# GpSimd normalises per chunk of tokens: one two-scalar operation instead of two broadcast operations, with the planner's constants that go with it

## The chip, the cores and the metric

The kernel runs on one core of a Trainium2 chip. The metric is the device time of one execution in microseconds (us); lower is better. The engines are TensorE (PE, with its weight load PEld), VectorE (DVE), ScalarE (ACT), GpSimd (POOL) and SyncE (SP, which issues DMAs).

## The reference

The input x has 32 sequences of 256 tokens with 128 features. Three residual steps follow one another: a feed-forward network at half weight, an attention, and the same feed-forward network again.

```
x = x + 0.5 * ffn(layernorm(x))
x = x + attn(layernorm(x))          # 16 heads of 8 features; inside: layernorm(ctx + x) * gamma + beta
x = x + 0.5 * ffn(layernorm(x))
```

The ffn has three layers, 128 (with its negative) to 512, 512 to 512 and 512 to 128, whose weights are +1 or -1, with a ReLU after the first two. The layernorm subtracts the mean of a token and multiplies with `rsqrt(var + eps)`. So every token is normalised four times: ahead of the first ffn, ahead of the attention, inside the attention, and ahead of the second ffn.

## The kernel before

The work is cut into 16 units of 512 tokens (two sequences each). A unit is a tile of 128 partitions by 4 chunks by 128 features; a chunk is 128 tokens, one to a partition. For each unit `u` the kernel calls `norm_first` and `first` (norm and first ffn), `norm_attn` and `project` (norm, query, key and value), then for each of its two sequences `b` `maxima` and `shift` (scores and their row maximum), `weigh` (scores again, exponential, product with the values) and `context` (division, residual, the inner layernorm), and last `second` (norm, second ffn, store). In the ffn every hidden value is held as a sum of two fp16 numbers, high and low (`relu_split`, lines 661 to 667).

None of these functions issues an instruction at once. Each calls `op`, which notes a node with its engine, a cost, what it reads and writes, and a rank. `_Plan.simulate` then plays all nodes through a list scheduler and writes down one fixed order for each engine; the chip runs that order. The rank is the due time of a node in score steps: a unit has 16 ranks (`UNIT`), because it has 16 groups of score matmuls, one a rank. The constants at the top of the file enter there:

- `B0`, `BA`, `BP`, `BW`, `B1`, `P0`, `P1`, `P2`, `BB`, `AHEAD`, `RUSH`: the rank at which each part of a unit starts.
- `TURN_X`, `TURN_C`: TensorE's transposes get an even rank plus this number (line 632 for the normalised tile, line 921 for the context).
- `SKIP0`, `SKIP`, `UNTIL`: score groups run strictly by rank. Other TensorE work may be taken ahead of its turn, up to `SKIP0` ranks ahead of the oldest group left, and up to `SKIP` ranks once that group's rank passes `UNTIL` (line 243).
- `CAST`, `BIAS`, `BIAS2`: costs and thresholds by which a `relu_split` is turned from DVE to POOL. In `relief`, ACT writes the ReLU a second time in fp32 (`full`, line 666) and POOL subtracts (line 661). In `divert`, ACT writes only `full` (line 667), and POOL makes the high part (CAST, line 667) and the low part (line 661).
- `QF`, `QK`, `QL`: for which units the normalising is `quick`, that is, done on DVE: the first ffn of units below `QF`, the attention norm of units below `QK`, and the context and second ffn of the last `QL` units.

TensorE has three ways of cutting its array: score groups use four row strips ("R"), the product with the values four column strips ("C", lines 877 and 423), the transposes the whole array ("D", lines 420, 630, 921). The ffn and projection products (kind "F", function `dense`) take the cut that is set at that moment: L423 in strips, L420 whole.

`normalize` (lines 590 to 618) first takes the statistics of each chunk on DVE (L603, L604: mean and variance into `mv`), then on POOL `ve = (var + eps) / scale^2` (L605) and `rs = ve ^ -0.5` (L607). If not `quick`, POOL then does the whole tile in two operations with broadcast operands (L617 subtracts the means, L618 multiplies with `rs`); it works on 4 chunks in the ffn and attention norms (tiles `fxn`, `axn`, 128x512) and on 2 in the context (tile `z`, 128x256). If `quick`, DVE does one operation for each chunk with two scalars per partition (L612), and `ve` and `rs` are made for two chunks at a time. `turned` then transposes the tile (L630) and splits it (L633, L634).

Of the kernel before, what the change touches and what calls it, by code (L numbers as in the profile page):

```python
# [41 lines left out]
ALU = mybir.AluOpType  # L42
# [7 lines left out]
EPS = 1e-5  # L50
# [4 lines left out]

PT, NXN = 5, 5

QF, QK = 1, 1

QL = 1  # L60

UNIT = 16
B0, BA, BP, BW, BV, B1 = -30, -10.627, -6.547, 13, 4, 42.462

P0, P1, P2, SLOW = 16.003, 17.354, 16, 1

TURN_X, TURN_C = 1.5, 1.5  # L70

WARM = 14

BB = 15.813

RUSH, AHEAD = -0.12, 4.08

SKIP0, SKIP, UNTIL = 10.311, 2.868, 28.215

FAR = 19.64  # L80

HOLD = (0, 0.0, 0.0)

CAST = 1.0

WAIT = 0.057

# [4 lines left out]

AFTER, REACH = (0.165, 0.085, 0.11, 0.04, 0.0), (0.053, 0.033, 0.037, 0.08, 0.05)

BIAS = 1.115

BIAS2 = 0.714
PE, DVE, ACT, POOL, SP = range(5)


# [19 lines left out]
class _Plan:  # L120
# [11 lines left out]
    def op(self, eng, cost, emit, r=(), w=(), rank=0.0, kind="D", rows=0, lag=None, alt=None, rush=False):  # L132
        x = _Node()
        x.n, x.eng, x.cost, x.emit, x.rank, x.kind, x.rows = len(self.nodes), eng, cost, emit, rank, kind, rows
        x.lag, x.alt, x.tiling = lag, alt, "D"
        x.then, x.avail, x.start, x.rush = [], 0.0, None, rush
        x.pair = None
        needs = set()
        for k in r:
            if k in self.wrote:  # L140
                needs.add(self.wrote[k])
        for k in w:
            if k in self.wrote:
                needs.add(self.wrote[k])
            needs.update(self.read.pop(k, ()))
        for k in r:
            self.read.setdefault(k, []).append(x)
        for k in w:
            self.wrote[k] = x
        needs.discard(x)  # L150
        x.needs = list(needs)
        for y in x.needs:
            y.then.append(x)
        x.bufs = []
        for k in (*r, *w):
            b = k[0] if isinstance(k, tuple) else k
            if isinstance(b, _Buf) and b not in x.bufs:
                x.bufs.append(b)
                b.left += 1
        self.nodes.append(x)  # L160
        return x

    def simulate(self):
# [12 lines left out]
        def fits(x, also=()):  # L176
            want = {}
            for b in (*x.bufs, *also):
                if not b.held:
                    want.setdefault(b.tag, set()).add(b)  # L180
            return all(used.get(tag, 0) + len(bs) <= next(iter(bs)).bufs for tag, bs in want.items())
# [86 lines left out]
        def relief(now, best):  # L268

            nonlocal left  # L270
            for x in sorted((x for x in ready[DVE] if x.alt and x.avail <= now + 1e-9), key=lambda x: (x.rank, x.n)):
# [5 lines left out]
                other = max(now + act + 0.2, max(free[POOL], now) + wait) + pool  # L277
                if other > max(free[DVE], now) + before + x.cost + BIAS:
                    continue
# [23 lines left out]
        def divert(x, now):  # L303
# [7 lines left out]
            wait = sum(y.cost for y in ready[POOL] if (y.rank, y.n) < (x.rank, x.n))  # L311
            if max(free[POOL], end + 0.2) + wait + cost + sub > max(free[DVE], end) + before + low.cost + BIAS2 or not fits(x, [full]):
                return
# [76 lines left out]
def tile_macaron(ctx: ExitStack, tc: tile.TileContext, x, Wq, bq, Wk, bk, Wv, bv, gamma, beta, k0, k1, k2, s0, s1, s2, out):  # L390
    nc = tc.nc
    plan = _Plan(tc)
    op = plan.op
    B, S, D = x.shape
# [16 lines left out]
    def buf(pool, shape, dt, tag, bufs, name):  # L411
        return _Buf(pool, shape, dt, tag, bufs, name)
# [12 lines left out]
    def bc(ap, n):  # L425
        return ap.broadcast_to([ap.shape[0], ap.shape[1], n])
# [67 lines left out]
    scale = const.tile([P, 3], F32, name="scale")  # L494
# [5 lines left out]
    def projections():  # L500
# [15 lines left out]
        s = lambda emit, w, rank=-700: op(SP, 0.42, emit, w=w, rank=rank, lag=4.5)  # L516
        v = lambda cost, emit, r, w, rank=B0 + BB: op(DVE, cost, emit, r=r, w=w, rank=rank)
        for i, (W, b) in enumerate(((Wq, bq), (Wk, bk), (Wv, bv))):
# [11 lines left out]
        def permute(dst, src, eng):  # L530
            to = dst.rearrange("p (r d c e) -> p c r d e", r=R, d=HD, c=2)
            of = src.rearrange("p (c r e d) -> p c r d e", c=2, r=R, e=2)
            for c in range(2):
                eng(to[:, c], of[:, c])

        op(ACT, 0.4, lambda: permute(pid, ident, nc.scalar.copy), r=["ident"], w=["pid"], rank=B0 + BB)
        op(PE, 0.2, lambda: nc.tensor.transpose(bp.t, bound, ident), r=["bound", "ident"], w=[bp], rank=B0 + BB + 0.1)
        v(0.2, lambda: nc.vector.tensor_reduce(top[:, 0:1], bp.t, AX.X, ALU.max), [bp], ["top"])
        v(0.1, lambda: nc.vector.tensor_scalar(top[:, 1:2], top[:, 0:1], 320.0, 1e-30, ALU.mult, ALU.max), ["top"], ["top"])
        op(POOL, 0.5, lambda: nc.gpsimd.tensor_tensor(top[:, 2:3], top[:, 1:2], nhalf[0:3, 0:1], ALU.pow), r=["top", "nhalf"], w=["top"], rank=B0 + BB)  # L540

        v(0.1, lambda: nc.vector.tensor_scalar(top[:, 3:4].bitcast(I32), top[:, 2:3].bitcast(I32), 0x7F800000, None, ALU.bitwise_and), ["top"], ["top"])
        v(0.1, lambda: nc.vector.tensor_scalar(diag, ident[0:3, 0:3], top[:, 3:4], None, ALU.mult), ["ident", "top"], ["diag"])
        op(PE, 0.2, lambda: nc.tensor.matmul(sp.t, ones, diag, start=True, stop=True), r=["ones", "diag"], w=[sp], rank=B0 + BB + 0.2)
        v(0.1, lambda: nc.vector.tensor_scalar(scale, sp.t, 2.0**13, None, ALU.mult), [sp], ["scale"])
        for i in range(3):
            op(ACT, 0.22, lambda i=i: nc.scalar.activation(ws[:, i, :], ws[:, i, :], AF.Identity, scale=scale[:, i : i + 1]), r=[("ws", i), "scale"], w=[("ws", i)], rank=B0 + BB)
        v(0.2, lambda: nc.vector.reciprocal(inv, scale[:, 0:2]), ["scale"], ["inv"])
# [41 lines left out]
    def normalize(dst, src, tag, n, rank, scale=1.0, quick=False):  # L590

        of = lambda: src[0].t[:, src[1] : src[1] + n]
        srcs = [(src[0], src[1] + t) for t in range(0, n, 2)]
        mv = buf(small, [P, n, 2], F32, f"mv{tag}", 4, f"mv_{tag}")
        ve = buf(small, [P, n], F32, f"ve{tag}", 4, f"ve_{tag}")
        rs = buf(small, [P, n, 1], F32, f"rs{tag}", 4, f"rs_{tag}")
        step = 2 if quick else n
        for a in range(0, n, step):
            part = slice(a, a + step)
            ts = range(a, a + step)  # L600
            for t in ts:
                st = buf(small, [P, 6], F32, f"st{tag}", 4, f"st_{tag}_{t}")
                op(DVE, 0.195, lambda t=t, st=st: nc.vector.bn_stats(st.t, of()[:, t, :]), r=[srcs[t // 2]], w=[st], rank=rank)  # L603
                op(DVE, 0.085, lambda t=t, st=st: nc.vector.bn_aggr(mv.t[:, t, :], st.t), r=[st], w=[(mv, t)], rank=rank)  # L604
            op(POOL, 0.27, lambda part=part: nc.gpsimd.tensor_scalar(ve.t[:, part], mv.t[:, part, 1], EPS, 1.0 / scale**2, ALU.add, ALU.mult),  # L605
               r=[(mv, t) for t in ts], w=[(ve, a)], rank=rank)
            op(POOL, 0.35 + 0.2 * step, lambda part=part: nc.gpsimd.tensor_tensor(rs.t[:, part, 0], ve.t[:, part], nhalf[:, part], ALU.pow),  # L607
               r=[(ve, a), "nhalf"], w=[(rs, a)], rank=rank)
        mvs = [(mv, t) for t in range(n)]
        if quick:  # L610
            for t in range(n):
                op(DVE, 0.26, lambda t=t: nc.vector.tensor_scalar(dst.t[:, t, :], of()[:, t, :], mv.t[:, t, 0:1], rs.t[:, t, :], ALU.subtract, ALU.mult),  # L612
                   r=[srcs[t // 2], (rs, t // 2 * 2), (mv, t)], w=[(dst, t)], rank=rank)
        else:
            dsts = [(dst, t) for t in range(n)]
            cost = 0.2 + 0.2 * n
            op(POOL, cost, lambda: nc.gpsimd.tensor_tensor(dst.t, of(), bc(mv.t[:, :, 0:1], D), ALU.subtract), r=[*srcs, *mvs], w=dsts, rank=rank)  # L617
            op(POOL, cost, lambda: nc.gpsimd.tensor_tensor(dst.t, dst.t, bc(rs.t, D), ALU.mult), r=[(rs, 0)], w=dsts, rank=rank)  # L618

    def turned(xn, tag, name, n, rank):  # L620

# [34 lines left out]
    def relu_split(hi, lo, m, ps, w, rank):  # L656
# [3 lines left out]
        def low(of):  # L660
            return lambda: nc.gpsimd.tensor_tensor(lo.t[:, m, :], of.t, hi.t[:, m, :], ALU.subtract)  # L661
# [4 lines left out]
           alt=(0.09 + w / 1280, lambda: nc.scalar.activation(full.t, ps.t, AF.Relu), ps, full, 0.1 + w / 500, low(full)))  # L666
        h.pair = (l, lambda: nc.scalar.activation(full.t, ps.t, AF.Relu), full, CAST * w / 512, lambda: nc.gpsimd.tensor_copy(hi.t[:, m, :], full.t),
                  0.1 + w / 500, low(full))
# [61 lines left out]
    def second(u, b):  # L730
# [3 lines left out]
        rank = at(u) + (b or 0) * UNIT / 2  # L734
        norm_ffn(("ffn1", u, b), (xs[u], part), n, rank - AHEAD, u >= NU - QL)
        dsts = ffn(("ffn1", u, b), (xs[u], part), n, rank, span * n / NT)
# [216 lines left out]
    for u in range(NU):  # L953
# [10 lines left out]
        for b in range(2):  # L964
            weigh(u, b)
            context(u, b, u >= NU - QL)
            if u == NU - 1:
# [34 lines left out]
```

## Time and profile before

| what | us |
|---|---|
| median of 3 runs (lowest, highest) | 687.96 (687.93, 688.52) |
| the profiled execution's own time | 689.46 |
| its span, first to last instruction | 687.6 |
| PE busy | 659.8 (96%) |
| DVE busy | 581.1 (85%) |
| ACT busy | 543.1 (79%) |
| POOL busy | 497.3 (72%) |
| mean granted TensorE clock | 0.995 |

The span is one execution as the hardware profiler saw it. The profiled execution is 1.50 us longer than the median, and 1.86 us of its time lie outside the span. A busy share is an average over the whole span; the stretches differ. An answer by windows gives the busy time of each engine in a stretch of the span. The chain of waits is the work that ended last, followed backwards.

### The profile page before, as it was taken

To read this page: it belongs to the slowest core of one execution; us is meant where nothing else is said; L and a number is where in the kernel's file an instruction comes from. 1 tells how busy PE (TensorE), PEld (TensorE's weight loads), DVE (VectorE), ACT (ScalarE), POOL (GpSimd) and SP (SyncE) were. 2 spreads that over 40 slices of the span, in tenths; PEclk is the share of its full clock that TensorE was granted. 3 is DMA by queue.
4 is the path that set the end of the run, shared out by engine and by line. 5 is a ranking of instruction groups with operands and counts; after the bars stand their busy time and mean duration, and the time that the engine had idled before them with its cause. 6 is when DMAs were issued, how large, how long until landed. Compare 5 with 4: busy or idle time off the path is not lost.

```text
span 687.6 us, 28926 instructions
## 1 busy us (share of the span) xinstructions
PE 659.8 (96%) x12596; PEld 344.6 (50%) x12596; DVE 581.1 (85%) x1194; ACT 543.1 (79%) x871; POOL 497.3 (72%) x685
## 2 busy tenths in 40 slices
PE   7998978999999999999999999999999999999996
PEld 4544533545455554555455454555445454544455
DVE  7789887998989798898979889897988888889484
ACT  3546887788889888888978888897889787868953
POOL 6875596688686868768686877868686785865643
PEclk9999998999999999999999999999999999999999
DMA  7222200203011030301102030200203021300000
GB/s 222 76 79 80 64 23 3 83 5 98 5 49 54 3 98 4 100 4 58 46 5 97 3 99 5 76 27 16 86 5 97 4 74 30 96 4 20 5 17 31
DMA packets 33391, 33.59 MB, mean 49 GB/s; under 512 B 4992, under 2 KB 29056, under 8 KB 33264
## 3 DMA queue, kind: packets, MB, share of 16 engines
q1 hardware_dynamic: 31520, 30.89, 14.3%
q8 instruction: 99, 1.62, 1.0%
q10 hardware_dynamic: 1744, 0.85, 0.4%
q14 instruction: 28, 0.23, 0.1%
HBM read 18.58 MB, written 13.14 MB: 46 GB/s over the span
## 4 chain that ended last, share of the span: by engine, by line
PE 82%; DVE 7%; ACT 4%; POOL 3%; DMA 2%; issue 1%; SPq 0%; ACTq 0%; POOLq 0%
PE p_None L423 18%; PE p L423 17%; PE cx L877 16%; PE sc L895 9%; PE p L420 6%; DVE nm L836 4%; PE p_None L420 3%; PE nat L825 3%; ACT pt L907 2%; PE tp L921 2%; PE pq L423 2%; PE pq L420 1%; PE pv L423 1%; PE t L630 1%; PE t_None L630 1%
## 5 line engine op out<-in xcount | busy, mean ns | idle before, releaser
L836 DVE TENSOR_REDUCE nm<-nat 128x4 f32<-128x1024 f32 x256 | 310.5, 1216 | 27.4 <-PE nat L825 22.0
L907 ACT ACTIVATE pt<-sc,esc 128x1024 f32<-128x1024 f32 x256 | 285.2, 1116 | 54.7 <-PE nat L825 45.2
L423 PEld LDWEIGHTS <-w 128*32 128x32 f16 x3976 | 97.4, 96 | 102.4 <-issue 28.9
L877 PE MATMUL cx<-pt,vaug 128*32 128x256 f32 x2048 | 137.2, 385 | 0.0
L895 PE MATMUL sc<-qs,ks 32*128 32x256 f16 x1024 | 103.2, 274 | 6.7 <-ACT pt L907 4.9
L825 PE MATMUL nat<-ks,qs 32*128 32x256 f16 x1024 | 101.7, 274 | 3.9 <-ACT pt L907 1.8
L877 PEld LDWEIGHTS cx<-pt,vaug 128*32 128x32 f32 x2048 | 58.6, 110 | 44.7 <-issue 12.3
L423 PE MATMUL p<-h1h,w 128*32 128x512 f16 x796 | 78.5, 383 | 0.0
L423 PE MATMUL p<-h1l,w 128*32 128x512 f16 x796 | 78.0, 380 | 0.0
L423 PE MATMUL p_None<-h1h_None,w 128*32 128x512 f16 x744 | 73.6, 382 | 0.1
L423 PE MATMUL p_None<-h1l_None,w 128*32 128x512 f16 x744 | 73.0, 379 | 0.0
L895 PEld LDWEIGHTS <-ks 32*128 32x128 f16 x1024 | 31.7, 92 | 75.0 <-issue 70.7
L661 POOL TENSOR_TENSOR h2l_None<-full,h2h_None 128x512 f16<-128x512 f32 x27 | 31.5, 1168 | 27.6 <-ACT full L666 27.3
L661 POOL TENSOR_TENSOR h2l<-full,h2h 128x512 f16<-128x512 f32 (+1 forms) x36 | 40.8, 1134 | 11.5 <-ACT full L666 10.8
L663 ACT ACTIVATE h1h<-p 128x512 f16<-128x512 f32 (+1 forms) x68 | 37.3, 577 | 13.6 <-PE p L420 9.0
L825 PEld LDWEIGHTS <-qs 32*128 32x128 f16 x1024 | 31.3, 92 | 29.7 <-issue 28.7
L663 ACT ACTIVATE h2h<-p 128x512 f16<-128x512 f32 (+1 forms) x56 | 32.3, 576 | 15.7 <-PE p L420 11.8
L664 DVE SCALAR_TENSOR_TENSOR h2l_None<-p_None,h2h_None 128x512 f16<-128x512 f32 x33 | 22.7, 687 | 25.7 <-ACT h2h_None L663 25.6
L420 PEld LDWEIGHTS <-w 128*128 128x128 f16 x326 | 30.1, 98 | 28.5 <-issue 10.5
L664 DVE SCALAR_TENSOR_TENSOR h1l<-p,h1h 128x512 f16<-128x512 f32 (+1 forms) x61 | 39.4, 663 | 1.1 <-ACT h1h L663 0.8
L663 ACT ACTIVATE h2h_None<-p_None 128x512 f16<-128x512 f32 x56 | 33.4, 596 | 6.0 <-PE p_None L420 4.9
L423 PE MATMUL p_None<-xT_None,w 128*32 128x512 f16 x480 | 35.4, 380 | 0.0
(163 smaller groups left out, 1471.7 us busy)
## 6 DMA issues: line engine op xcount, KB each, us to landing
dr<-qkhl SPq DMA_DIRECT2D x32, 256.0 KB, 2.0
qs<-dr SPq DMA_DIRECT2D x48, 128.0 KB, 3.3
ks<-dr SPq DMA_DIRECT2D x48, 128.0 KB, 2.6
out_dram<-x SPq DMA_DIRECT2D x15, 256.0 KB, 3.0
x<-in_L_attn_x_dram SPq DMA_DIRECT2D x14, 256.0 KB, 6.1
dm<-mr SPq DMA_DIRECT2D x32, 16.0 KB, 2.5
qs<-dm SPq DMA_DIRECT2D x32, 16.0 KB
qs<-nought SPq DMA_DIRECT2D x13, 32.0 KB
```

Source lines behind the costliest of these rows:

```text
L420: nc.tensor.matmul(to, w, of, start=start, stop=stop)
L423: nc.tensor.matmul(to[32 * r : 32 * r + 32], w[:, 32 * r : 32 * r + 32], of, start=start, stop=stop)
L630: nc.tensor.transpose(pt.t[:, bass.ts(t, P)], xn.t[:, t, :], ident)
L661: return lambda: nc.gpsimd.tensor_tensor(lo.t[:, m, :], of.t, hi.t[:, m, :], ALU.subtract)
L663: h = op(ACT, 0.09 + w / 1280, lambda: nc.scalar.activation(hi.t[:, m, :], ps.t, AF.Relu), r=[ps], w=[(hi, m)], rank=rank)
L664: l = op(DVE, 0.08 + w / 985, lambda: nc.vector.scalar_tensor_tensor(lo.t[:, m, :], ps.t, 0.0, hi.t[:, m, :], ALU.max, ALU.subtract), r=[p ...
L825: nc.tensor.matmul(nat.t[:, ii, qc, :], Q[32 * r : 32 * r + 32, g, b * S + qc * P : b * S + qc * P + P], K[32 * r : 32 * r + 32, g, b * S ...
L836: op(DVE, 1.141, lambda g=g, pr=pr, nat=nat: nc.vector.tensor_reduce(nm.t[:, :, 2 * pr : 2 * pr + 2, g].rearrange("p q i -> p i q"), nat.t ...
L877: nc.tensor.matmul(cx.t[32 * r : 32 * r + 32, g // 2, :], V[:, 2 * b + kc, 4 * (g // 2) + r, 16 * (g % 2) : 16 * (g % 2) + 32], pts[g, r / ...
L895: nc.tensor.matmul(sc.t[:, ii, kc, :], K[32 * r : 32 * r + 32, g, b * S + kc * P : b * S + kc * P + P], Q[32 * r : 32 * r + 32, g, b * S : ...
L907: op(ACT, 1.012, lambda pt=pt, sc=sc: nc.scalar.activation(pt.t, sc.t, AF.Exp, scale=esc), r=[sc, "esc"], w=[pt], rank=rank - RUSH, rush=True)
L921: nc.tensor.transpose(tp.t[:, qc, 8 * c : 8 * c + 8, :].rearrange("p h n -> p (h n)"), cxT.t[:, c, bass.ts(qc, P)], ident)
```

## The change

`normalize` loses its two-operation branch. POOL now does what DVE did in the quick branch, one operation for each chunk, `(x - mean) * rs` with the chunk's two scalars, and each writes its chunk alone, so that what reads a chunk waits for that chunk. The planner's cost of it is `EACH`. With it come other values of the planner's constants; they change ranks, thresholds and the set of quick units, and so the order of every engine's queue.

```diff
-QF, QK = 1, 1
-QL = 1
+QF, QK = 3, 1
+QL = 0
...
-B0, BA, BP, BW, BV, B1 = -30, -10.627, -6.547, 13, 4, 42.462
-P0, P1, P2, SLOW = 16.003, 17.354, 16, 1
-TURN_X, TURN_C = 1.5, 1.5
+B0, BA, BP, BW, BV, B1 = -30, -11.353, -5.977, 13, 4, 42.462
+P0, P1, P2, SLOW = 16.003, 17.354, 15.993, 1
+TURN_X, TURN_C = 0.5, 1.5
...
-BB = 15.813
-RUSH, AHEAD = -0.12, 4.08
-SKIP0, SKIP, UNTIL = 10.311, 2.868, 28.215
+BB = 16
+RUSH, AHEAD = 0.144, 4.08
+SKIP0, SKIP, UNTIL = 10.602, 2.868, 20.746
...
-CAST = 1.0
+CAST = 0.62
+EACH = 0.4
...
-BIAS = 1.115
-BIAS2 = 0.714
+BIAS = 1.143
+BIAS2 = 0.765
...
-            op(POOL, 0.27, lambda part=part: nc.gpsimd.tensor_scalar(ve.t[:, part], mv.t[:, part, 1], EPS, 1.0 / scale**2, ALU.add, ALU.mult),
+            op(POOL, 0.21, lambda part=part: nc.gpsimd.tensor_scalar(ve.t[:, part], mv.t[:, part, 1], EPS, 1.0 / scale**2, ALU.add, ALU.mult),
...
-        mvs = [(mv, t) for t in range(n)]
-        if quick:
-            for t in range(n):
-                op(DVE, 0.26, lambda t=t: nc.vector.tensor_scalar(dst.t[:, t, :], of()[:, t, :], mv.t[:, t, 0:1], rs.t[:, t, :], ALU.subtract, ALU.mult),
-                   r=[srcs[t // 2], (rs, t // 2 * 2), (mv, t)], w=[(dst, t)], rank=rank)
-        else:
-            dsts = [(dst, t) for t in range(n)]
-            cost = 0.2 + 0.2 * n
-            op(POOL, cost, lambda: nc.gpsimd.tensor_tensor(dst.t, of(), bc(mv.t[:, :, 0:1], D), ALU.subtract), r=[*srcs, *mvs], w=dsts, rank=rank)
-            op(POOL, cost, lambda: nc.gpsimd.tensor_tensor(dst.t, dst.t, bc(rs.t, D), ALU.mult), r=[(rs, 0)], w=dsts, rank=rank)
+        e, eng, cost = (DVE, nc.vector, 0.26) if quick else (POOL, nc.gpsimd, EACH)
+        for t in range(n):
+            op(e, cost, lambda t=t: eng.tensor_scalar(dst.t[:, t, :], of()[:, t, :], mv.t[:, t, 0:1], rs.t[:, t, :], ALU.subtract, ALU.mult),
+               r=[srcs[t // 2], (rs, t // step * step), (mv, t)], w=[(dst, t)], rank=rank)
```

## The prediction

> **What bounds the kernel now.** I read the page first (busy shares and slices), then the busy time by windows, then the chain of waits, then POOL's groups by form, last the timelines of single stretches.
>
> ```profile
> PE 659.8 (96%) x12596; PEld 344.6 (50%) x12596; DVE 581.1 (85%) x1194; ACT 543.1 (79%) x871; POOL 497.3 (72%) x685
> ```
>
> POOL is the least busy of the four. By windows:
>
> ```profile
> core 0: us, PE busy (x) PEld busy (x) DVE busy (x) ACT busy (x) POOL busy (x), PEclk, DMA share, GB/s
> 43.00:64.00 21.00, 18.44 (x386) 8.98 (x389) 20.40 (x25) 10.91 (x22) 11.81 (x14) 1.00 0.21 65
> ...
> 86.00:116.00 30.00, 23.52 (x329) 10.25 (x321) 24.18 (x51) 22.47 (x31) 25.48 (x34) 0.89 0.06 15
> ...
> 600.00:640.00 40.00, 36.82 (x658) 17.52 (x657) 34.29 (x58) 31.20 (x43) 24.93 (x39) 1.00 0.06 21
> ...
> 660.00:687.60 27.60, 20.98 (x185) 14.81 (x178) 14.83 (x37) 9.71 (x25) 10.57 (x18) 0.99 0.06 20
> ```
>
> ```profile
> 251.73:291.40 39.67, 39.67 (x828) 20.68 (x831) 34.82 (x72) 33.99 (x55) 30.58 (x42) 1.00 0.14 45
> ```
>
> The last line is one unit of the middle. From about 120 to 530 us every such period of 39.67 us has PE busy for all of it: 410 / 39.67 = 10.3 periods in which a faster POOL buys nothing by itself. PE idles 27.8 us in all (687.6 - 659.8), all at the ends: some 9 in the first 65 us, 6.5 in 86 to 116, 1.5 in 569 to 600, 3.2 in 600 to 640, 6.6 from 660 on. A gain must come from there, or from what PE itself spends in the middle.
>
> **Price of the new operation.**
>
> ```profile
> L617 POOL TENSOR_TENSOR z<-y,mv_c 128x256 f32<-128x256 f32 x30 | 18.4, 613 | 2.2
> ...
> L617 POOL TENSOR_TENSOR fxn<-x,mv_f 128x512 f32<-128x512 f32 x15 | 15.7, 1047 | 0.5
> ...
> L484 POOL TENSOR_SCALAR w<-k1s,sc 128x512 f16<-128x512 uint8 x2 | 1.7, 844 | 2.6 <-DVE sc L477 2.6
> ...
> L849 POOL TENSOR_SCALAR ns<-nm 128x32 f32<-128x32 f32 x32 | 9.5, 297 | 32.5 <-DVE nm L836 32.1
> ```
>
> No row has a POOL operation with two scalars per partition on 128x128. The two L617 forms (613 and 1047 ns) give 1.70 ns an element and a fixed 0.18 us. L484 is the nearest row, a tensor_scalar with one scalar per partition: (844 - 180) / 512 = 1.30 ns an element, so 0.18 + 128 x 1.30 = 0.35 us; I take that. From below POOL's CAST (397 ns at 256 elements, 609 at 512) gives 0.29; from above the L617 line gives 0.40, and L849, if its surplus grew with the elements ((297 - 180) / 32 = 3.7 ns), 0.65. Four chunks cost 1.40 against 2 x 1.04 = 2.08, two cost 0.70 against 2 x 0.61 = 1.23. A middle unit has three norms of four chunks and two contexts: 3 x 0.68 + 2 x 0.53 = 3.1 us off POOL's 30.6; at 0.29 it is 4.1, at 0.65 it is 1.6 more. The break-even is 0.52 us a chunk.
>
> The Trainium skill (GPSIMD Engine Reference, 3.1 Elementwise) lets a light one-input body run at 1.03 cycles of 1.2 GHz an element, which with the fixed 0.18 would be an estimate of 0.29 us a chunk and the 4.1 us; L484's 1.30 ns is slower than that, so the trace's row stands. A rule against the change is in Perfetto Trace Analysis, Optimizing Scalar/DVE Operations (written for DVE and ScalarE): group into larger operations. Here splitting two into four pays the fixed 0.18 twice more, 0.36 of the 2.08, and the saved pass is worth more; both are in the sum.
>
> **What POOL's relief is worth.** In the middle, nothing directly. Turned into DVE work: one `divert` costs POOL 0.61 + 1.16 = 1.77 us and takes 0.69 off DVE at no ACT cost, so 3.1 us carry 1.7 of them, 1.2 us of DVE a unit. `CAST` (0.38 less) and `BIAS2` (0.05 more) let the planner do so more readily. It counts only where DVE is on the chain:
>
> - 43 to 116 us: DVE is full in 43 to 64, but with row maxima (L836), which cannot move; only some of the low parts after 62 us can. Two units' worth is 2.4; I take 1.5 off (0 to 2.5).
> - 569 to 640 us: on the chain there stand low parts on DVE at 599.72, 600.40, 610.24, 614.24 and 629.24, 0.59 + 0.67 + 0.69 + 0.69 + 1.22 = 3.9 us, while POOL idles 15 of 40 us. I take half, 2.0 off (0 to 3.9).
>
> **The window constants.** The third window above is a hole. The chain there:
>
> ```profile
> 98.45 0.96 POOL rs_f L607
> 99.41 0.70 POOL y L936
> 100.11 0.94 POOL fxn L618
> 101.05 0.14 issue
> 101.19 0.30 POOL ns L849
> ```
>
> This looks as if POOL caused it, but L849's own input is there only at 100.4 (the row maximum of 99.17 lasts 1.22), so a faster POOL gains at most 0.8 here; I take 0.5. The hole itself is the planner's: between 93 and 108 us PE is given score groups and value products only, since the oldest rank passes `UNTIL` = 28.2 and the window drops from 10.3 to 2.9 ranks, 7.44 ranks without ffn work. The new values drop it by 10.602 - 2.868 = 7.73 ranks, some 7.5 ranks earlier. So the hole moves and stays: 6.5 x 7.73 / 7.44 = 6.8, 0.3 on (from 3 off to 2.5 on: in the old hole the granted clock fell to 0.50 between 105 and 110 us, and a moved one may escape or repeat that).
>
> **The quick units.** `QF` = 3 sends the first norms of units 1 and 2 to DVE, 2 x 4 x 0.34 = 2.8 us, ahead of unit 0's ffn by rank, and splits `ve` and `rs` in halves on POOL. DVE idles some 9.5 us in the first 40; PE's own products hold the chain for 7.08 us from 12.26. Behind the new operations queue unit 0's low parts, for which PE waits. 0.5 on (1 off to 2.8 on). `QL` = 0 sends the last unit's context and norm to POOL:
>
> ```profile
> 665.91 1.32 POOL L661 TENSOR_TENSOR h2l_None<-full,h2h_None 128x512 f16<-128x512 f32 x1 [1.25 <-ACT full L666]
> ```
> ```profile
> 666.25 1.26 DVE L941 TENSOR_TENSOR x<-x,z 128x256 f32<-128x256 f32 x1
> ...
> 667.76 0.67 DVE L664 SCALAR_TENSOR_TENSOR h2l_None<-p_None,h2h_None 128x512 f16<-128x512 f32 x1
> ```
>
> On DVE, L941 takes 1.26 us while POOL runs (a like operation, L940, takes 0.42), and the low part behind it, ready at 667.07, starts 0.69 late; PE waits for it until 668.49. On POOL three adds and a product cost 4 x 0.81 start to start, the two chunks 0.70, against 0.42 + 0.60 + 0.43 + 0.42 + 1.26 on DVE: some 0.8 longer, but past the low part. 0.7 off (2 off to 1.5 on).
>
> **The middle.** A whole-array group between strip work costs PE 0.15 us at each change of cut:
>
> ```profile
> 269.85 0.44 PE ta L630 x4
> ...
> 273.75 0.59 PE tp L921 x4
> ...
> 290.82 0.58 PE t L630 x4
> 291.41 0.33 PE cx L877
> ```
>
> Four transposes take 0.44 when what stands before them is whole too, 0.58 after strips, and cx then 1.00 instead of 0.86. The period holds three such extra changes, 0.44 us. `TURN_X` = 0.5 moves the transposes of L630 from odd intervals, where the ffn products can be whole with them, to even ones, where a value product (cx, strips) always stands. At best all extras go (-0.44 a period, -4.5 over 10.3); with one extra for each L630 group and none for tp the period stays; sandwiched on both sides with tp once, 3 x 0.29 + 0.15 = 1.02 gives +0.58 (+6.0). I take 0, as nearest to one extra each.
>
> **Sum.** 0.5 - 1.5 - 0.5 + 0.3 - 2.0 - 0.7 + 0 = -3.9 us. The profiled execution would go from 689.46 to 685.5, the median from 687.96 to 684.0.
>
> **Rivals.**
> - *The transposes cost PE more changes of cut* (slower). For it: PE has no idle time in the middle, so 0.15 us counts 10.3 times each. Against: the planner charges for changes too (0.108) and can choose the cut of F products. It decides from 3.9 / 10.3 = 0.38 us a period; at +0.58 the time is 687.96 - 3.9 + 6.0 = 690.1. Chance 0.24.
> - *Nothing moves*: POOL was never late, the diverts do not land on the chain, the ends cancel. Time 687.9. For it: POOL idle 190 us. Against: low parts on the chain at 600 to 640. Chance 0.10.
> - *The middle shortens too*: the three extras go and the hole keeps its clock, 684.0 - 4.5 - 2 (of the hole's 3) = 677.5. Chance 0.16.
> - *The chunk operation costs 0.65*: POOL 1.6 heavier a unit, the reliefs of 1.5, 2.0 and 0.5 are lost: 688.0; it falls together with the second.
>
> **How the numbers follow.** The forecast proper, 684.0, has 0.50. Its own bounds do not all add up at once; the larger ones, 2.5 to 3 either way, give some 681 to 687. The range reaches to the third rival below (677.5) and past the first above, 677 to 691. About 0.2% (1.4 us) is what can be told from no change: faster means below 686.6, the forecast and the third rival, 0.66; within 0.2% 0.10; slower 0.24.
>
> **What the changed profile would show.** L617 and L618 gone, a POOL TENSOR_SCALAR of 128x128 near 0.35 us; POOL's CAST rows (L667) more in number and L664 on DVE fewer; a period in the middle of 39.67 us with PE full; a hole of PE some 15 us earlier; L941 on POOL to the end. It is wrong if the period differs by over 0.2 us either way, since that times 10.3 outweighs half the sum, or if the chunk operation is over 0.52 us.

## The result, and the profile after

The changed kernel takes 741.26 us (median of 4 runs, 738.97 to 741.91) against 687.97 (687.93 to 688.52) of the kernel before in the same comparison: 1.0767 times as long, 95% interval 1.0743 to 1.079. 684.0 had been forecast, 677 to 691 as the range. Its profiled execution took 741.26 us with a span of 739.5.

From the page of the kernel after, the busy shares and the chain by engine:

```profile
PE 678.2 (92%) x12341; PEld 347.8 (47%) x12341; DVE 579.3 (78%) x1182; ACT 543.8 (74%) x866; POOL 575.4 (78%) x800
...
POOL 41%; PE 39%; DVE 9%; ACT 6%; issue 4%; DMA 0%; SPq 0%; POOLq 0%; ACTq 0%; DVEq 0%
```

POOL was to lose some 3 us a unit; it gained 78 us in all (497.3 before), and it holds 41% of the chain of waits, where before it held 3% and PE 82%. POOL's busy *share* went up by only six points, so the share does not show what happened. The windows of the kernel after do (columns as before). The first line is the stretch after the first units' start, the second one period of the middle, the third the counterpart of 600 to 640 us, the last the end:

```profile
50.20:71.20 21.00, 17.88 (x336) 8.21 (x329) 19.29 (x23) 9.39 (x20) 14.62 (x19) 1.00 0.20 65
...
254.33:297.21 42.88, 40.49 (x785) 20.85 (x785) 35.44 (x72) 33.89 (x53) 33.59 (x47) 1.00 0.13 41
651.40:691.40 40.00, 36.55 (x658) 16.95 (x650) 31.11 (x51) 32.67 (x45) 28.69 (x43) 1.00 0.06 17
711.90:739.50 27.60, 20.25 (x169) 14.54 (x166) 11.00 (x28) 8.71 (x23) 13.00 (x22) 0.94 0.06 20
```

The stretches at the ends look much as they did. The middle does not: a period lasts 42.88 us in place of 39.67, and PE, which had been busy for all of it, idles 2.39; the other 0.8 us is longer PE work (40.49). To place the loss, take as the mark of a unit the start of ScalarE's first copy of its values (`vaug<-pv`). Unit 0 has it at 35.4 us before and 42.6 after (+7.3 before rounding); from there to unit 3's it is 89.2 and 95.5 (+6.3); ten periods on, 396.4 and 429.9 (+33.6); two more, 74.5 and 78.7 (+4.2); the rest to the end 92.2 and 92.8 (+0.6). Together that is 51.9, the difference of the spans.

POOL's groups by form, of the kernel after, say why:

```profile
L613 POOL TENSOR_SCALAR z<-y,mv_c,rs_c 128x128 f32<-128x128 f32 x64 | 50.6, 796 | 3.0
L613 POOL TENSOR_SCALAR fxn_None<-x,mv_f,rs_f 128x128 f32<-128x128 f32 x60 | 47.1, 795 | 1.0
```

One chunk takes 0.80 us, not 0.35, so four take 3.13 where the two old operations took 2.08. And the chain of waits of the kernel after, in a period of the middle (start, length, what), shows what that does to PE:

```profile
278.87 0.20 POOL ve_c L607
...
279.98 1.59 POOL z L613 x2
...
287.95 3.13 POOL axn L613 x4
...
293.32 1.21 POOL fxn_None L613 x2
...
296.13 0.80 POOL fxn_None L613
296.94 0.23 POOL mt L846
297.16 0.04 issue
297.21 0.23 PE pm L851
```

For 18.3 us, from 278.87 to 297.16, every link is POOL or its issue: a context norm, an attention norm, an ffn norm, and at their end `mt`, the shift of the row maxima, on which PE's `pm` waits, and with it what stands behind it in PE's order. Yet POOL idles 9 us of the same period elsewhere. The waits of the kernel after agree (us in total, times, longest); before, the first of these rows was 4.0 us:

```profile
PEld L851 <- POOL mt L846: 26.4, 18, 2.3
PEld ta L626 <- POOL axn L613: 22.6, 45, 1.3
```

### The profile page after: what moved, and what is told of

Read it like the earlier page. It is cut to its first block, busy times and chain, and to the rows that moved or that the text cites. A ratio compares the mean times of both kernels' runs of the same rounds, so it can differ in the third digit from the quotient of the medians.

```text
span 739.5 us, 28490 instructions
## 1 busy us (share of the span) xinstructions
PE 678.2 (92%) x12341; PEld 347.8 (47%) x12341; DVE 579.3 (78%) x1182; ACT 543.8 (74%) x866; POOL 575.4 (78%) x800
## 4 chain that ended last, share of the span: by engine, by line
POOL 41%; PE 39%; DVE 9%; ACT 6%; issue 4%; DMA 0%; SPq 0%; POOLq 0%; ACTq 0%; DVEq 0%
PE p L425 8%; PE cx L873 6%; POOL axn L613 6%; PE p_None L425 6%; POOL fxn_None L613 5%; POOL z L613 4%; DVE nm L832 3%; PE sc L891 3%; PE p L422 3%; POOL h1l L657 3%; POOL h2l_None L657 3%; ACT pt L903 3%; POOL rs_a L609 2%; PE nat L821 2%; PE p_None L422 2%
## 5 line engine op out<-in xcount | busy, mean ns | idle before, releaser
L903 ACT ACTIVATE pt<-sc,esc 128x1024 f32<-128x1024 f32 x256 | 285.3, 1117 | 68.6 <-PE nat L821 53.3
L425 PEld LDWEIGHTS <-w 128*32 128x32 f16 x3840 | 93.5, 96 | 90.8 <-issue 28.1
L873 PEld LDWEIGHTS cx<-pt,vaug 128*32 128x32 f32 x2048 | 61.8, 110 | 46.4 <-issue 13.8
L425 PE MATMUL p_None<-h1l_None,w 128*32 128x512 f16 x712 | 70.0, 379 | 0.0
L613 POOL TENSOR_SCALAR z<-y,mv_c,rs_c 128x128 f32<-128x128 f32 x64 | 50.6, 796 | 3.0
L932 POOL TENSOR_TENSOR y<-y,axn 128x256 f32<-128x256 f32 x32 | 23.3, 728 | 36.8 <-DVE y L930 36.0
L422 PEld LDWEIGHTS <-w 128*128 128x128 f16 x360 | 35.1, 104 | 33.0 <-issue 13.2
L613 POOL TENSOR_SCALAR axn<-x,mv_a,rs_a 128x128 f32<-128x128 f32 x60 | 47.0, 794 | 1.4
L660 DVE SCALAR_TENSOR_TENSOR h2l<-p,h2h 128x512 f16<-128x512 f32 (+1 forms) x37 | 23.8, 644 | 30.9 <-ACT h2h L659 30.0
L613 POOL TENSOR_SCALAR fxn_None<-x,mv_f,rs_f 128x128 f32<-128x128 f32 x60 | 47.1, 795 | 1.0
L613 POOL TENSOR_SCALAR fxn<-x,mv_f,rs_f 128x128 f32<-128x128 f32 x56 | 44.0, 795 | 0.5
```

Of the source, the lines that this page charges most:

```text
L422: nc.tensor.matmul(to, w, of, start=start, stop=stop)
L425: nc.tensor.matmul(to[32 * r : 32 * r + 32], w[:, 32 * r : 32 * r + 32], of, start=start, stop=stop)
L613: op(e, cost, lambda t=t: eng.tensor_scalar(dst.t[:, t, :], of()[:, t, :], mv.t[:, t, 0:1], rs.t[:, t, :], ALU.subtract, ALU.mult), r=[src ...
L660: l = op(DVE, 0.08 + w / 985, lambda: nc.vector.scalar_tensor_tensor(lo.t[:, m, :], ps.t, 0.0, hi.t[:, m, :], ALU.max, ALU.subtract), r=[p ...
L873: nc.tensor.matmul(cx.t[32 * r : 32 * r + 32, g // 2, :], V[:, 2 * b + kc, 4 * (g // 2) + r, 16 * (g % 2) : 16 * (g % 2) + 32], pts[g, r / ...
L903: op(ACT, 1.012, lambda pt=pt, sc=sc: nc.scalar.activation(pt.t, sc.t, AF.Exp, scale=esc), r=[sc, "esc"], w=[pt], rank=rank - RUSH, rush=True)
```

## Experiments

Theory: the chunk operation costs twice what the order was booked with, and in a fixed order that makes PE wait for POOL in the middle. Rival: the new constants (and what else the planner orders anew) cost it. "Period" is the distance of the marks in the middle (their mean where they alternate), 39.67 us before.

| kernel | us | ratio to before (95%) | unit 0's mark | period |
|---|---|---|---|---|
| after | 741.26 | 1.0767 (1.0743 to 1.079) | 42.6 | 42.9 |
| norm_only | 722.94 | 1.0506 (1.0484 to 1.0527) | 37.2 | 42.1 |
| consts_only | 705.13 | 1.0259 (1.0234 to 1.0283) | 42.7 | 40.6 |
| each_true | 719.53 | 1.0456 (1.0432 to 1.048) | 41.8 | 40.2 |
| after_cheap | 697.95 | 1.0135 (1.0115 to 1.0155) | 42.7 | 40.1 |
| norm_booked | 708.10 | 1.029 (1.0266 to 1.0314) | 35.2 | 40.7 |
| qf3 | 692.91 | 1.0061 (1.0046 to 1.0076) | 39.3 | 39.67 |
| turnx | 701.88 | 1.0189 (1.017 to 1.0209) | 36.3 | 40.73 |
| after_mended | 705.63 | 1.0263 (1.0243 to 1.0283) | 38.0 | 41 |
| add_only | 696.83 | 1.0125 (1.0111 to 1.0139) | 36.6 | 40.45 |
| ql0 | 687.14 | 0.9982 (0.997 to 0.9993) | 35.6 | 39.67 |
| add_ql0 | 696.37 | 1.0122 (1.0107 to 1.0138) | 36.8 | 40.45 |
| same_order_sub | 737.82 | 1.072 (1.0705 to 1.0734) | 40.1 | 42.99 |
| same_order_cheap | 690.35 | 1.0034 (1.0022 to 1.0046) | 36.6 | 39.68 |
| same_order_ql0 | 690.00 | 1.0029 (1.0017 to 1.004) | 36.5 | 39.68 |

**The price by itself.** A kernel of little else than POOL operations on 128 partitions, in several forms and sizes:

```diff
+g.tensor_scalar(t, xf[:, 0:128], a, b, ALU.subtract, ALU.mult)   # two_ptr: two scalars per partition
+g.tensor_scalar(t, xf[:, 0:128], a, b, ALU.add, ALU.mult)        # two_ptr_add
+g.tensor_scalar(t, xf[:, 0:128], a, None, ALU.subtract)          # one_ptr_sub
+g.tensor_scalar(t, xf[:, 0:128], -0.5, b, ALU.add, ALU.mult)     # imm_ptr
```

> This kernel leaves the whole network out: it runs six of each of 17 GpSimd forms and one VectorE form on tiles in SBUF, one form after another, and writes sums of them. Theory A (the chunk operation itself costs 0.80 us, whatever stands around it): the two-scalar 128x128 form takes 0.75 to 0.85 us here too. Rival (it is slow in the network only because VectorE holds something that GpSimd needs): it takes 0.30 to 0.40 us here. If the price goes by elements, 32, 64, 256 and 512 of them give about 0.33, 0.49, 1.42 and 2.66 us. Open beforehand: whether it is the second operation (then the one-operation forms take about half), the pointer scalars (then the immediate forms are cheap), the subtraction (then add is cheap), or fp32 against uint8 (then the fp32 form of 512 elements takes well over 0.84 us).

POOL's timeline of this kernel, pairs of one operation each (start, length of the pair):

```profile
14.24 1.59 POOL L67 TENSOR_SCALAR two_ptr<-xs,sc 128x128 f32<-128x128 f32 x2
15.81 0.88 POOL L72 TENSOR_SCALAR two_ptr_add<-xs,sc 128x128 f32<-128x128 f32 x2
16.67 1.18 POOL L77 TENSOR_SCALAR one_ptr_sub<-xs,sc 128x128 f32<-128x128 f32 x2
...
21.25 0.74 POOL L97 TENSOR_SCALAR imm_ptr<-xs,sc 128x128 f32<-128x128 f32 x2
```

From start to start, subtract-then-multiply takes 0.79 us a chunk, add-then-multiply 0.43 with the same operands, and with an immediate 0.37. At 32, 64, 256 and 512 elements subtract-then-multiply takes 0.46, 0.56, 1.2 and 2.06: 0.36 fixed and 3.3 ns an element. At 512 elements an immediate add and a multiplication by a scalar take 0.68, a third of that. So at the same size and with the same operands the pair of arithmetic operations sets the price. The operands count too, but less: with two immediates subtract-then-multiply takes 0.62. The slow form is as slow here, in a kernel without the network, as in the changed kernel: theory A of this run came out.

**Which part costs the time.** norm_only has the constants of before and the new branch with its booking; consts_only the reverse.

```diff
 # norm_only, on the kernel before: the new branch of normalize, and
+EACH = 0.4
 # consts_only, on the kernel after: the old branch of normalize (L617, L618 with cost 0.2 + 0.2 * n)
```

> Before's constants and quick units, with only the chunk operation put in, booked at 0.40 us. Theory A (the operation's price and its booking are the loss): GpSimd gets 3 x (3.18 - 2.08) + 2 x (1.59 - 1.23) = 4.0 us more a unit, its order is made for 0.40 and so it is late; 715 to 745 us. Theory B (the planner's new constants are the loss, above all TURN_X): 686 to 695 us.

> After's constants and quick units, with the two broadcast operations of before left in place and booked at their old costs (0.2 + 0.2 a chunk). Theory A: near before or a little faster, 680 to 690 us, with PE full in the middle. Theory B: over 715 us.

Against the 688.02 beside them, the operation with its booking costs 34.9 us, as theory A expected, and the constants alone 17.1, which neither A nor B had expected. Both theory and rival hold a part; the operation has the larger one.

**Booking, and a cheap operation.** each_true only books the truth; after_cheap runs the cheap pair in the changed kernel's own order; norm_booked is norm_only with the true booking.

```diff
 # each_true (on after) and norm_booked (on norm_only)
-EACH = 0.4
+EACH = 0.78
 # after_cheap (on after)
-... ALU.subtract, ALU.mult)
+... ALU.add if eng is nc.gpsimd else ALU.subtract, ALU.mult)
```

> After with EACH at 0.78, the measured price start to start, instead of 0.40. Theory A1 (the wrong booking is the loss, because the fixed order makes others wait behind GpSimd): most comes back, 690 to 705 us. Theory A2 (the added GpSimd work is the loss): 725 to 741 us. Theory B: 735 us or more.

> After with one word changed: GpSimd's chunk operation adds the mean where after subtracts it (so the normalised values are not the network's), because the price run showed add-and-multiply at 0.43 us start to start and subtract-and-multiply at 0.79. Every order, wait and booking is after's; only the price comes down to what is booked (0.40). Theory A (the loss over the constants alone, 36 us, is the price against the booking): it falls to the time of the run with after's constants and the old operations, 700 to 708 us, with a middle period near 40.6. Rival (the new waits of single chunks, not the price): it stays above 725 us. Had the prediction's price been its only error, 684 us.

> Before's constants and quick units, the chunk operation put in and booked at its true 0.78 us instead of 0.40 (the run with 0.40 took 722.9 us, period 42.1). Theory A1 (a wrong booking is what costs: GpSimd has room for 4 us more a unit if the order knows of it): period 39.7 to 40.3, 692 to 702 us. Theory A2 (the work itself): period above 41.5, 715 us or more.

With 0.45 us a chunk (mean in its profile) and nothing else altered, the changed kernel needs 697.95: 43 of its 53 us go with the price, a little more than theory A expected, and far from the rival's 725. With the price kept and only the booking put right, 719.53, 22 us less: in the order that the planner makes when it knows the price the period is 40.2 in place of 42.9. each_true and norm_booked both lie between what their theories A1 and A2 expected.

**The constants one by one.** Each is a one-line change to the kernel before.

```diff
-QF, QK = 1, 1
+QF, QK = 3, 1
 # turnx
-TURN_X, TURN_C = 1.5, 1.5
+TURN_X, TURN_C = 0.5, 1.5
 # ql0
-QL = 1
+QL = 0
```

> Before with QF = 3 alone: the first norms of units 1 and 2 on VectorE at the start. Theory S (QF costs the start: VectorE's normalising runs into GpSimd's memsets, as the 3.41 us for four of them at 19.05 us in the run with after's constants shows against 0.34 each alone): the first projection copy, at 35.4 us in before, comes at 40 to 43, and the time is 692 to 696 us. Rival (BB, BA or BP moved the start): the first copy stays at 35 to 37 us and the time at 686 to 690.

> Before with TURN_X = 0.5 alone. Theory B (transposes among strip work cost TensorE changes of cut): a period of 39.9 to 40.7 in the middle and 691 to 703 us. Rival (the 0.9 us a period that after's constants cost in the middle come from the other constants): period 39.5 to 39.8, 686 to 690 us.

> Before with QL = 0 alone: the last unit's context and norm on GpSimd with the two broadcast operations. The prediction took 0.7 us off for it. Theory: the tail from the last projection copy to the end is 92.2 us in before and 88.5 in the run with after's constants; if QL is the reason the time is 684 to 687 us. Rival (the other constants shorten the tail): 687.5 to 690 us.

`QF` = 3 costs 4.5 us, 4.0 of them at unit 0's mark, which at 39.3 falls just short of the 40 to 43 of its theory. `QL` = 0 gains 1.2 us, between what theory and rival expected, and it is the only kernel of the study that beats the one before, by 0.18%. `TURN_X` = 0.5 costs 13.5 us, as theory B expected. Two links of its chain of waits, and one steady period by windows:

```profile
316.68 0.59 PE ta L630 x4
...
320.00 0.59 PE tp L921 x4
```
```profile
287.70:328.43 40.73, 40.32 (x876) 20.25 (x872) 35.65 (x73) 32.52 (x53) 30.23 (x42) 1.00 0.14 44
```

All five whole-array groups of a period now cost 0.59; before, three of them cost 0.44. That makes 0.45 us of the 1.06 that a period loses. PE's work has grown by 0.65 in all (40.32 against 39.67), and the other 0.41 is idle time, in which PE waits once for the low part `h1l` on DVE. Some periods ahead of the steady ones are longer still (41.8).

**A mended change.** The cheap pair on a mean that DVE negates first: as the changed kernel with the two costly constants put back, and alone on the kernel before, without and with `QL` = 0.

```diff
+op(DVE, 0.08, lambda part=part: nc.vector.tensor_scalar(neg.t[:, part], mv.t[:, part, 0], -1.0, None, ALU.mult), ...)
-... mv.t[:, t, 0:1], rs.t[:, t, :], ALU.subtract, ALU.mult)
+... neg.t[:, t : t + 1], rs.t[:, t, :], ALU.add, ALU.mult)      # EACH = 0.43
 # after_mended: on after, also QF, QK = 1, 1 and TURN_X, TURN_C = 1.5, 1.5
 # add_only: on before;  add_ql0: add_only with QL = 0
```

> After with three things put right: the chunk operation adds a negated mean (made on VectorE, one small operation a norm) and is booked at 0.43; TURN_X is 1.5 again and QF 1 again; all else is after's. Theory (loss = price against booking + TURN_X + QF, nothing else): first projection copy back near 35 us, period 39.7 to 39.9, and with the shorter tail seen in the run with the cheap operation (4 us) 682 to 689 us. Rival (other constants of after cost as well): 692 us or more; the first copy at 38 or later would name BB, BA or BP.

> Before's constants and quick units with the chunk operation in its cheap form (adds a negated mean from VectorE), booked at 0.43. Theory: GpSimd has 4 x 0.43 instead of 2 x 1.04 us a norm and VectorE 5 small operations more a unit, TensorE stays full in the middle: period 39.6 to 39.9, 684 to 689 us. Rival (a new order from the same planner loses by chance what the old one had, as each of the changed orders so far did): period over 40.2, 695 us or more.

> The cheap chunk operation with before's constants and QL = 0: the two that could gain together. 681 to 688 us if both hold; as much as the run without QL = 0 if the tail does not depend on it.

after_mended missed its expectation by some 17 us: its periods alternate between 39.1 and 42.7. Its rival came out, that other constants cost as well; unit 0's mark, at 38.0, stands where that expectation would name `BB`, `BA` or `BP`, but these were not tried one by one. add_only loses 0.78 us a period, though POOL is relieved (467.8 busy), and so its rival came out too; add_ql0 gains 0.5 on it. So neither the price nor `TURN_X` and `QF` were the whole story: either the chunk operation costs something beside its length, or the order that is made anew loses, or the negation on DVE does. This last one is no small operation. It was booked at 0.08, and in add_only the 75 of them take 32.9 us. One in a middle period:

```profile
314.54 1.07 DVE L609 TENSOR_SCALAR ng_f<-mv_f 128x4 f32<-128x4 f32 x1
```

The same operation takes 0.17 at 289.35. At 314.54 POOL is in an operation of 1.27 us that began at 314.31, and the negation ends with it. DVE's `xTa` comes right behind, at 315.53, and PE waits 0.31 for `xTa`: that is all the time for which PE idles in this period.

**The order held fast.** The planner keeps its two old nodes with their old costs, so PE, DVE, ACT and SP run the old order instruction by instruction (the traces record DVE's 1194 and ACT's 871 operations in the order of before); only what the nodes emit on POOL differs, the negation among it.

```diff
-op(POOL, cost, lambda: nc.gpsimd.tensor_tensor(dst.t, of(), bc(mv.t[:, :, 0:1], D), ALU.subtract), ...)
-op(POOL, cost, lambda: nc.gpsimd.tensor_tensor(dst.t, dst.t, bc(rs.t, D), ALU.mult), ...)
+op(POOL, cost, lambda: nc.gpsimd.tensor_scalar(neg.t, mv.t[:, :, 0], -1.0, None, ALU.mult), ...)
+op(POOL, cost, chunks, ...)   # the n chunk operations: add form (same_order_cheap), subtract form (same_order_sub)
```

> The kernel before, every instruction of PE, DVE, ACT and SP in its old order and with the old booked costs; only what GpSimd issues in the two places of a norm differs: in place of the subtraction it negates the means (128x4 or 128x2), in place of the product it runs the four (two) chunk operations in the form add, multiply at 0.43 each. A norm of four costs 0.2 + 1.72 = 1.9 us in place of 2.08. Theory (the 0.78 us a period that add_only lost come from the order that the planner makes anew, not from the operation): the period stays at 39.67, first copy near 35.4, 686.5 to 688.5. Rival (the operation itself costs, by holding up DVE or by releasing the chunks late): a period near 40.45 and 694 to 697.

> The same with the chunk operation of the change (subtract, multiply, 0.79 each): 0.2 + 3.16 = 3.4 us in place of 2.08 for a norm of four, 1.8 in place of 1.23 for a context of two, some 5 us a period more on GpSimd, whose idle time there is 9 us, with all other engines in the old order. Theory (a static order made for a shorter operation makes PE wait for GpSimd, even with room to spare): a period of 40.2 to 41.5, 694 to 707, less than the 722.9 of the order that was made for 0.40 a chunk. Rival (the 9 us of idle time take it up, and norm_only lost by its new order): 39.67 to 39.9, 688 to 691.

> The first kernel of this call with QL = 0, so GpSimd also takes the last unit's context and norm. Theory (the end gains 1.2 us as it did alone, and the chunk operation is shorter there too): 685.5 to 687.2, first copy 35.5, period 39.67, the last 91 us or less. Rival (the operation costs in the middle): 693 to 696.

A period by windows, first of same_order_cheap, then of same_order_sub:

```profile
242.70:282.40 39.70, 39.70 (x831) 20.62 (x823) 34.80 (x71) 34.06 (x56) 30.29 (x53) 1.00 0.15 45
```
```profile
259.50:302.50 43.00, 40.29 (x831) 20.70 (x823) 34.85 (x72) 34.29 (x55) 35.86 (x53) 1.00 0.13 42
```

With the cheap pair the middle is untouched: PE full, 39.68 a period. The pair has no hidden cost there. So what add_only lost in the middle came from what else it changed, the new order and the negation on DVE: 0.31 us a period is the wait behind the negation, the rest (0.47) more PE work. A new order with the negation on POOL was not tried, so how much is left for the order is open. With the subtract pair, in the same order, the period is 42.99 and the time 737.82: 49.6 us over the 688.22 beside it. Not one instruction of the other engines had been moved. This is nearly as much as the changed kernel's whole loss, and it went past the 694 to 707 that the theory expected, let alone the rival's 691 that trusted in POOL's idle 9 us.

PE's own waits in that period of same_order_sub (us in total, times, longest):

```profile
PE p_None L423 <- POOL h1l_None L667: 1.2, 1, 1.2
PE pm L861 <- POOL mt L856: 1.2, 1, 1.2
```

With 0.3 for a transpose they make the 2.7 us for which PE idles; the other 0.6 of the 3.3 is longer PE work. The reason can be read in the kernel before. Its timelines of POOL (first row) and PE (second), around 275 us:

```profile
274.35 0.25 POOL L850 TENSOR_TENSOR mt<-ns,mt 128x32 f16<-128x32 f32 x1
```
```profile
275.48 0.22 PE L855 MATMUL pm<-ident,mt 128*32 128x128 f16 x1
```

`mt` is done at 274.60, PE takes it at 275.48: the slack is 0.88 us (0.67 up to the load of `mt` as weights, at 275.27). Ahead of it POOL works from 264.13 to 274.60 with one wait, of 0.25, and two whole norms of four chunks lie in that stretch. Each grows from 2.08 to 3.4 us (3.14 and the negation), 2.6 in all, and PE then waits; in same_order_sub the wait of `pm` is 18.2 us in 12 waits, of its weight load 25.8 in 17. The second release, again POOL and then PE:

```profile
288.54 1.17 POOL L661 TENSOR_TENSOR h1l_None<-full,h1h_None 128x512 f16<-128x512 f32 x1
```
```profile
290.44 0.39 PE L423 MATMUL p_None<-h1l_None,w 128*32 128x512 f16 x4
```

Here the slack is 0.73 us (289.71 to 290.44), and ahead of it POOL works without a gap from 279.49, one context norm and one norm of four among it. They grow by 0.6 and 1.3 us, 1.9 together, and 1.9 - 0.73 is the 1.2 us that PE waits.

same_order_cheap is 2.1 us slower than before, although its middle is not. Its profile does not settle why, since the profiled execution is as long as that of before (689.48 against 689.46). It starts 1.3 us later: the 28 opening warm-up products are recorded with 6.09 us against 4.79, before any altered operation has run (4.8 to 6.3 in the profiles of this study). It has made that up by unit 3's mark, ahead of which the granted clock of before fell (0.50 between 105 and 110 us) and its own did not (1.00). same_order_ql0 missed: its last part is 91.4 us against 92.6 in same_order_cheap, about what ql0 gained there (1.1), but it starts as late, and its granted clock fell to 0.58 between 105 and 110 us.

## Why the prediction was wrong, step by step

**The price of the chunk operation: the step that failed first.** 0.35 was taken as nearest row, with bounds of 0.29 and 0.65; measured 0.79 to 0.80, beyond both. The nearest row was nearest in kind of instruction only. L484 adds an immediate and multiplies, which is the cheap pair (0.68 us at 512 elements in the run by itself, 0.84 in the trace). L849, set aside as the far bound, came nearer, but by luck: it is a lone multiplication, and its surplus of 3.7 ns an element, beside 3.3 measured, hangs on a fixed part of 0.18; with the 0.36 measured its 0.297 us would leave none. So the break-even of 0.52 was passed. The Trainium skill's light body of 1.03 cycles an element (GPSIMD Engine Reference, 3.1 Elementwise) had given 0.29; 3.3 ns are 4.0 cycles of its 1.2 GHz, so the measurement decides against it for this pair.

**"The reliefs are lost: 688.0": the step that cost most.** The fourth rival had the right mechanism, a chunk over 0.52, and priced it at nothing, because in the middle POOL's time was taken to be free in both directions. That a *faster* POOL buys nothing there is right, as same_order_cheap shows. That a slower one costs nothing is wrong by 3.3 us a period: in the old order PE waits at two releases whose slack was 0.88 and 0.73 us, and the 9 us of idle time lay elsewhere. Ten such periods are 33 of the 52 us.

**The planner's booking.** The prediction did not weigh what `EACH` = 0.40 does to the order if the operation is dearer. In the changed kernel it is worth 22 us (each_true, whatever else the new order changes included).

**The middle (`TURN_X`): 0 taken, bound +6.0, alone +13.5.** The sandwiched case, +0.58 a period in PE work, nearly came out (0.65 measured), where one extra for each L630 group, 0, had been taken; the step also lacked the idle time, 0.41 a period, in which PE waits for DVE's low part, and the longer periods ahead of the steady ones.

**The quick units.** `QF`: 0.5 taken, bound 2.8, measured 4.5; in qf3 two of the four pairs of moved chunks take 1.35 and 1.37 us a pair, where 0.34 a chunk had been counted. `QL`: -0.7 taken, -1.2 measured, with 91.1 us from unit 15's mark to the end in place of 92.2: the sole term that came out.

**Reliefs and the hole.** The planner did divert more (36 CASTs of 512 elements against 26), as forecast, but DVE's busy time fell by 1.8 us only, and nothing of the 3.5 shows: from 600 to 640 us PE idled 3.2, in its counterpart 3.5. The first three periods became 6.3 us longer, where the first relief and the two terms of the hole were to make them 1.7 shorter.

**Additivity.** The price in the old order (49.6) and the constants with the old operations (17.1) make 66.7, not 53.3: in the new order the price costs less. After the price is gone 10 us remain (after_cheap), of which `TURN_X` and `QF` alone would explain 17.9; so these parts don't add up either. What makes after_mended's periods alternate is open.

## What to carry to other kernels

In a statically ordered kernel, an engine's idle share is no reserve: look for the long stretches in which it runs without a gap, take the releases in them and at their ends, and read how long the waiting engine could have waited. A "nearest row" with other arithmetic operations missed the price here by a factor of 2.3; measure the operation by itself before an order is booked with it, a small helper operation too. And try the new operation in the old order first: it parts the price from what a new order brings in one run.

## What the runs showed of the hardware

On GpSimd, two scalars per partition with add and multiply run at 0.43 us for 128x128 fp32, with subtract and multiply at 0.79; even a lone subtraction or multiplication by a scalar (0.58 each) is slower than the add-and-multiply pair. Negating the mean first makes a chunk of the same normalisation about half as long; with the negation on GpSimd (0.23) a norm of four takes 2.0 us against 3.1, and the two old operations took 2.08.

GpSimd holds DVE up in consts_only's start. DVE's timeline, then POOL's:

```profile
19.05 3.41 DVE L614 TENSOR_SCALAR fxn<-x,mv_f,rs_f 128x128 f32<-128x128 f32 x4
```
```profile
18.65 1.38 POOL L578 MEMSET vaug<- 128x1536 f32 x1
19.97 0.95 POOL L579 MEMSET ks<- 128x1024 int32 x1
```

A third MEMSET follows from 20.86 to 21.80. The first two of the four quick chunks are recorded with 2.84 and 2.65 us and end at 21.89 and 21.95, right behind it; the last two take 0.33 each. So DVE stands still while POOL only fills memory, without a gap. The negation in add_only, 1.07 us in place of 0.17, ends together with POOL's operation in the same way (315.61 and 315.58). This is part of what the quick units cost at the start; that it is the whole of the 7.3 us there was not tried. The Trainium skill (SBUF — State Buffer, SBUF: two separate sides) calls the pair of ports that the two engines share an exclusive lock, held for a whole instruction by the one that starts first, where DVE's operation is in a two-port mode or has two inputs in SBUF. That DVE's operations end with POOL's, and are not slowed in proportion, agrees with a lock; in which mode they ran no profile here shows.
